# The last product with A taken by rows, and B split for the second pair already, in a two-block FFN kernel

## The chip, the cores and the metric

The kernel runs on one core of a Trainium2 chip. The metric is the device time of one execution in microseconds (us); the time of a version is the median of its runs. An execution is one launch that reads the inputs from HBM and leaves the output there.

## What is computed

The input x has 32 samples of 64 channels and 1024 positions. Two blocks follow one another, each of the form x + ffn(cond(x)). cond is four one-dimensional convolutions with styled weights (same, up, same, down). The first ffn is a gated mixture of low-rank experts, the second a dense layer with 4-bit weights:

```
def block0(x):                        # tokens: 2048 rows of 1024
    t = cond0(x, style)
    scores = t @ Wr.T                                  # 64 experts
    G = softmax of the 16 largest scores, 0 elsewhere
    h = einsum('nd,krd->nkr', t, A) * G[:, :, None]    # 64 experts x rank 16 = 1024
    return x + 2.0 * einsum('nkr,kdr->nd', h, B)
def block1(x):
    t = cond1(x, style)
    return x + t @ (scales * q - zeros) + bias
```

The change lies where block 0 passes from its product with A (and Wr) to its product with B.

## The kernel before, in words

**Pairs.** Two samples of 64 channels fill the 128 partitions, so there are 16 pairs. Three long loops run over them. The first (`for k in range(NP)`) makes the convolutions of block 0 for pairs ahead, and in `layer0` the product of pair k's tokens with A and Wr, the gates, and the gated h, which goes to DRAM (`hgd`). The second (`for p in range(NP)`) loads h of each pair, turns it with transposes (`turned_h`), multiplies it with B and adds the residual (`layer0b`). The third does block 1.

**Whole and split.** A product is done in one of two forms. In whole form it is an fp32 matmul; the profile has two records for each. In split form both sides are cut into an upper part (the top bits, `high`, L148) and a lower part, and three fp32r matmuls are summed: Q is upper x upper plus lower x lower, and D the product of the crossed parts (td = th - tl of the tokens, L872, and `crossed_weights` of the weights, L373). `joined` puts Q and D together. `WHOLE = (0, 1)` names the pairs that go in whole form, in both loops: the weights are loaded plain, and are split while pairs 0 and 1 run. Q and D each need a PSUM bank of their own, so a pair in split form holds two banks per chunk of columns, a whole one only one.

**Splitting the weights.** `split_weights` (L358 to L369) takes row k of the weights (128 of the 1024 contraction rows). For each half of its columns: a high on DVE (L148, into a tile of tag `hi`, of which there are three), the lower part by a subtraction on POOL (L365), and a copy of the high on ACT (L366); then, for the row, the crossing on DVE (L373). The result for row k lies in block k of the pool `wts`; A's split rows (`wa`), B's (`wb`) and others share these eight blocks, so row k of `wb` can be written only when row k of `wa` has been read for the last time. B itself comes plain into `cv` (`load_b`), over rooms that the convolutions of block 0 have left.

**Order.** The framework that assembles the kernel takes the instructions in the order of the program, with a place further ahead for what is ready earlier by its own estimate, fixes one queue per engine and sets the semaphores. Each engine then works its queue in that order. `tc.issue_after(x)` puts instructions behind x on x's engine. `layer0` and `layer0b` are generators: what stands between two `next(main)` in the loops is put between two parts of the product.

**Around the change.** In the last round of the first loop (pair 15) the product with A runs chunk by chunk: Q of chunks 0 and 1, D of both with the gates behind chunk 0, then chunk 2 (L973 to L999). Chunks 0 and 1 fill the four banks of tag `fps`, and chunk 2 takes two of these again. Then come the last three rows of B and the transposes of pair 0's h (L1330, L1331). In the second loop pairs 0 and 1 run whole from the plain B (`braw`), and `split_weights` is called for rows 0 to 3 in the first round and 4 to 7 in the second (L1365, L1366). Pair 2 is the first to use `wb`. The transposes pass through the three banks of tag `cps`. For the pairs from 2 on `turned_h` also makes tl and scales it (L864), and `crossed` makes td behind the pair before. `load_residual` fetches x of a pair: for whole pairs into a tile of tag `tl`, for others into `cv` at `O_Y + Y`, which overlaps rows 5 and 6 of the plain B.

Of the kernel before, what the change touches and what calls it, by code (L numbers as in the profile page):

```python
# [20 lines left out]
NP = B // 2  # L21
L = 1024
HL = L // 2
HQ = HL // 2 + 1
NC = L // P
H = 512
E = 64
# [35 lines left out]
def adaln_ffn_kernel(ctx: ExitStack, tc: tile.TileContext, t, out: bass.AP):  # L63
    nc = tc.nc
# [19 lines left out]
    def fpst(name):  # L84
        return fps.tile([P, H], F32, tag="fps", name=name)
# [66 lines left out]

    done, tbl, outers, uppers = {}, {}, {}, {}
    WHOLE = (0, 1)
    DIRECT = 4


# [744 lines left out]
    def layer0(p, ws):  # L902

        hs = wk.tile([P, AW], F32, tag="w4", name=f"hs{p}", bufs=3)
        key = f"x0_{p}"
        whole = p in WHOLE

        def joined(col, w, qd):
            dst = hs[:, col : col + w]
            if whole:  # L910
                nc.scalar.copy(dst, qd[0])
                return
            nc.scalar.activation(dst, qd[0], AF.Copy, scale=1.0 + 1.0 / RADIX)
            nc.vector.scalar_tensor_tensor(dst, qd[1], -1.0 / RADIX, dst, ALU.mult, ALU.add)

        ga = tiny.tile([P, E], F32, tag="ga", name=f"ga_{p}")

        def gates():
            s0 = hs[:, :E]
            m0 = tiny.tile([P, 8], F32, tag="m0", name=f"m0_{p}")  # L920
            m1 = tiny.tile([P, 8], F32, tag="m1", name=f"m1_{p}")
            s1 = tiny.tile([P, E], F32, tag="s1", name=f"s1_{p}")
            s2 = tiny.tile([P, E], F32, tag="s2", name=f"s2_{p}")
            nc.vector.max(m0, s0)
            nc.vector.match_replace(s1, m0, s0, LOW)
            nc.vector.max(m1, s1)
            nc.vector.match_replace(s2, m1, s1, LOW)
            nm = tiny.tile([P, 1], F32, tag="nm", name=f"nm_{p}")
            nc.vector.tensor_scalar_mul(nm, m0[:, 0:1], -1.0)
            ex = tiny.tile([P, E], F32, tag="ex", name=f"ex_{p}")  # L930
            nc.scalar.activation(ex, s0, AF.Exp, bias=nm)
            su = tiny.tile([P, 1], F32, tag="su", name=f"su_{p}")
            nc.vector.scalar_tensor_tensor(ga, s2, LOW, ex, ALU.is_equal, ALU.mult)
            nc.vector.reduce_sum(su, ga, axis=AX.X)
            nc.vector.reciprocal(su, su)  # L935
            done["gates"] = nc.vector.tensor_scalar_mul(ga, ga, su)

        def gated(c):
            a, b = CHUNKS[c]
            v = hs[:, E + a * R : E + b * R].rearrange("p (e r) -> p e r", r=R)  # L940
            g = ga[:, a:b].unsqueeze(2).to_broadcast([P, b - a, R])
            nc.gpsimd.tensor_tensor(v, v, g, ALU.mult)

        def chunk(c):
            a, b = CHUNKS[c]
            w = (b - a) * R + (E if c == 0 else 0)
            col = a * R + (E if c > 0 else 0)
            banks = [fpst(f"h{p}_{c}_{j}")[:, :w] for j in range(1 if whole else 2)]
            return banks, slice(col, col + w)

        def done_with(c, ch):
            product(ch, key, ws, at, D)
            joined(ch[1].start, ch[1].stop - ch[1].start, ch[0])

        if whole:

            three = [chunk(c) for c in range(3)]
            ks = (2, 3, 4, 5, 0, 1, 6, 7)
            for n, k in enumerate(ks):
                for ch in three:  # L960
                    product(ch, key, ws, at, Q, (k,), ks[0], ks[-1])
                if n in (0, 1, 2, 3, 5):
                    yield
            for c, ch in enumerate(three):
                done_with(c, ch)
            gates()
            yield
            for c in range(3):
                gated(c)
            nc.sync.dma_start(hgd[p], hs[:, E:])  # L970
            return

        two = []  # L973

        ks = tuple(range(6 if p == len(WHOLE) else NC))
        for c in range(2):
            two.append(chunk(c))
            product(two[c], key, ws, at, Q, ks)
            yield
        for c in range(2):  # L980
            if p == len(WHOLE):
                product(two[c], key, ws, at, D, ks)
            else:
                done_with(c, two[c])
                if c == 0:
                    gates()
            yield
        if p == len(WHOLE):
            for c in range(2):
                product(two[c], key, ws, at, Q, (6, 7))  # L990
                product(two[c], key, ws, at, D, (6, 7))
                joined(two[c][1].start, two[c][1].stop - two[c][1].start, two[c][0])
                if c == 0:
                    gates()
        ch = chunk(2)
        product(ch, key, ws, at, Q)
        yield
        done_with(2, ch)
        yield  # L999
        for c in range(3):  # L1000
            gated(c)
        nc.sync.dma_start(hgd[p], hs[:, E:])
# [4 lines left out]
        return hg  # L1007

    def turned_h(p, hg):
        whole = p in WHOLE  # L1010
        key = f"h{p}"
        th = tokens("th", f"th{key}", F32 if whole else F32R)
        toks[key] = [th] if whole else [th, tokens("tl", f"tl{key}")]
        for g in range(2):
            ps = cpst(f"ht{p}_{g}")
            for c in range(4):
                k = 4 * g + c
                nc.tensor.transpose(  # L1018
                    ps[:, c * P : (c + 1) * P], hg[:, k * P : (k + 1) * P], ident
                )  # L1020
            ks = slice(4 * g, 4 * g + 4)

            def d(v):
                return v[:, ks].rearrange("p a b -> p (a b)")

            if whole:
                nc.scalar.copy(d(th), ps)
            else:
                split(ps, lambda v: v, d(th), d(toks[key][1]), f"hh{p}_{g}")
        if not whole:  # L1030
            scaled_low(toks[key][1])
# [1 line left out]
    residual = {}  # L1033

    def load_residual(p):
        if p in WHOLE:
            v = tokens("tl", f"xres{p}", F32).rearrange("p a b -> p (a b)")
        elif p < NP - 1:
            v = cv[:, O_Y + Y : O_Y + Y + L]
        elif p < NP:  # L1040
            v = wk.tile([P, L], F32, tag="w4", name="xres", bufs=3)
        else:
            return
        nc.sync.dma_start(v, t["x"][p])
        residual[p] = v

    def layer0b(p, ws):

        whole = p in WHOLE
        key = f"h{p}"  # L1050
        xres = residual.pop(p)
        x1 = wk.tile([P, L], F32, tag="w4", name=f"x1_{p}", bufs=3)
# [20 lines left out]
        if p == NP - 1:  # L1073
            qds = [banks(c) for c in range(2)]

            for part in (Q, D):
                for k in range(4):
                    for ch in zip(qds, cols):
                        product(ch, key, ws, lambda k: k, part, (k,))
            yield  # L1080
            for ch in zip(qds, cols):
                product(ch, key, ws, lambda k: k, Q, range(4, NC))
                yield
            for c, ch in enumerate(zip(qds, cols)):
                product(ch, key, ws, lambda k: k, D, range(4, NC))
                joined(c, qds[c])
                if c == 0:
                    yield
        else:
            qds = [banks(c) for c in range(2)]  # L1090
            for ch in zip(qds, cols):
                product(ch, key, ws, lambda k: k, Q)
            for c, ch in enumerate(zip(qds, cols)):
                product(ch, key, ws, lambda k: k, D)
                joined(c, qds[c])
                yield
        if p not in WHOLE:
            load_residual(p + 1)
        nc.sync.dma_start(x1d[p].rearrange("p f j -> p (f j)"), x1)
        v = x1.rearrange("p (f j) -> p f j", f=4)  # L1100
# [185 lines left out]
    for k in range(NP):  # L1286
# [4 lines left out]
            outer_of(k + 2)  # L1291
        if last:
            hg = load_h(0)
        main = layer0(k, araw if k in WHOLE else wa)
        next(main)
        if k == 0:
# [28 lines left out]
        for fs in beside:  # L1325
            for f, *v in fs:
                f(*v)
            next(main)
        if last:
            load_b(range(5, NC), braw)  # L1330
            turned_h(0, hg)  # L1331
        elif k + 1 in WHOLE:
            outer(k + 1)
        if k + 2 < NP and k not in WHOLE:
            weights(k + 2)
# [8 lines left out]
        if not last:  # L1344
            crossed(f"x0_{k + 1}")

    hg = load_h(1)
    set1 = factors(1, cv[:, : 3 * AW], cv[:, 3 * AW : O_Y + Y])
    qw = None
    for p in range(NP):  # L1350
        if p + 1 < NP:
            turned_h(p + 1, hg)
        if p + 2 < NP:
            hg = load_h(p + 2)
        if p == NP - 1:
# [2 lines left out]
            tables_of(NP + 2)  # L1358
            outer_of(NP + 1)
            begin(NP + 1)  # L1360
        if p <= len(WHOLE):
            load_residual(p)
        main = layer0b(p, braw if p in WHOLE else wb)
        next(main)
        if p in WHOLE:  # L1365
            split_weights(braw, L, range(4 * p, 4 * p + 4), wb, "wb")  # L1366
        if p == 7:
            clear(1)
            clear_y([yv(0)])
# [112 lines left out]
```

## Time and profile before

| what | value |
|---|---|
| median of 3 runs | 908.21 us (907.2 to 909.05) |
| the profiled execution | 907.35 us, of which the span on the page is 905.3 us |
| granted TensorE clock over the span | 0.999 |
| pair 14's last product with A ends | 390.09 us |
| pair 15's product with A | 390.09 to 401.94 us |
| product with B, pairs 0 and 1 (whole) | 404.03 to 417.76 and 418.64 to 432.4 us |
| first and last subtraction for wb (POOL, L365) | 401.43 and 440.88 us |
| last crossing for wb (DVE, L373) ends | 442.14 us |
| pair 2 (the first in split form) | 433.0 to 446.5 us |
| pair 3 starts | 449.27 us |

Times within the profile are counted from the start of the span. PE is TensorE, PEld its weight loads, DVE is VectorE, ACT ScalarE, POOL GpSimd, SP the engine that issues most transfers. A row of a timeline gives the start, the length, the engine, the source line, the operation and its tiles; in brackets stands how long the engine had been idle before, and what ended that. The chain of waits goes back from the last instruction to whatever released each step.

### The profile page before, as it was taken

How to read it: one execution, taken by the hardware profiler on the slowest of the kernel's cores; microseconds unless marked ns; L12 is line 12 of the kernel's file. 1: busy time of each engine (PE TensorE's matmuls, PEld its weight loads, DVE VectorE, ACT ScalarE, POOL GpSimd, SP SyncE). 2: the span in 40 equal slices, each digit the busy share in tenths (PEclk: the TensorE clock that was granted, in tenths of full speed). 3: DMA queues.
4: the chain of work that ended last, by engine and by line, in shares of the span. 5: the costliest groups of instructions: out<-in, count | busy, mean ns of one | idle time of the engine just before them, and what ended most of it. 6: DMA issues, size and time to landing. Idle time of an engine off the chain costs nothing.

```text
span 905.3 us, 14844 instructions
## 1 busy us (share of the span) xinstructions
PE 876.4 (97%) x5133; PEld 785.8 (87%) x5133; DVE 707.1 (78%) x1450; ACT 328.4 (36%) x717; POOL 467.2 (52%) x603
## 2 busy tenths in 40 slices
PE   5999999999999999999899999999999999999997
PEld 4877789999999999994688888788899999999997
DVE  4565888888888888577986666569998899999986
ACT  6435433333333444333332221247233323333230
POOL 7325654444444444456571222433776767676673
PEclk9999999999999999999999999999999999999999
DMA  8521232222222222345376664456433243334311
GB/s 247 144 72 53 54 99 73 79 77 77 76 77 76 76 77 71 113 168 160 129 228 209 220 197 153 176 191 187 148 110 114 89 129 115 107 110 118 118 65 70
DMA packets 49738, 109.81 MB, mean 121 GB/s; under 512 B 13700, under 2 KB 22400, under 8 KB 49664
## 3 DMA queue, kind: packets, MB, share of 16 engines
q1 hardware_dynamic: 48704, 107.88, 38.3%
q10 hardware_dynamic: 960, 0.99, 0.5%
q8 instruction: 41, 0.67, 0.3%
q14 instruction: 33, 0.27, 0.1%
HBM read 70.97 MB, written 37.88 MB: 120 GB/s over the span
## 4 chain that ended last, share of the span: by engine, by line
PE 75%; DVE 12%; issue 5%; POOL 4%; DMA 2%; ACT 1%; DVEq 0%; POOLq 0%; ACTq 0%; SPq 0%
PE h L892 16%; PE o L892 15%; PE q L1143 12%; PE r L781 6%; PE f L608 6%; PE r L812 5%; PE c L732 5%; PE r L789 3%; PE g L585 2%; PE c L727 2%; DMA x1e<-dd 1%; PE ht L1018 1%; DVE cv L694 1%; DVE x L1063 1%; POOL wa L365 1%
## 5 line engine op out<-in xcount | busy, mean ns | idle before, releaser
L697 POOL TENSOR_TENSOR cv<-cv 128x256 f32<-128x256 f32 x120 | 77.8, 648 | 123.7 <-DVE su L935 72.6
L694 DVE TENSOR_TENSOR cv<-cv 128x257 f32<-128x257 f32 x120 | 99.7, 863 | 1.2 <-ACT cv L717 1.0
L729 ACT ACTIVATE yt<-c,be,al 128x257 f32<-128x257 f32 x56 | 31.7, 565 | 120.4 <-PE c L727 109.3
L1143 PE MATMUL q<-wq,thx 128*128 128x342 f32 x384 | 73.0, 331 | 1.6 <-ACT thx L850 1.6
L631 POOL TENSOR_TENSOR cv<-cv 128x256 f32<-128x256 f32 x60 | 56.1, 934 | 33.8 <-ACT cv L626 33.8
L1143 PE MATMUL q<-wq,tlx 128*128 128x342 f32 x384 | 72.4, 330 | 0.0
L892 PE MATMUL h<-wa,tdx 128*128 128x352 f32 (+1 forms) x336 | 71.9, 350 | 0.2 <-DVE wa L373 0.2
L797 DVE TENSOR_TENSOR rt<-r,tbl 128x256 f32<-128x256 f32 x60 | 25.1, 418 | 56.1 <-PE r L789 56.0
L608 PE MATMUL f<-gs,iw 128*128 128x128 f32 (+1 forms) x384 | 68.2, 327 | 0.2 <-issue 0.2
L781 PE MATMUL r<-cv 128*128 128x128 f32 x480 | 66.7, 282 | 0.9 <-POOL cv L631 0.5
L608 PEld LDWEIGHTS f<-gs,iw 128*128 128x128 f32 x384 | 61.8, 190 | 5.9 <-issue 0.5
L781 PEld LDWEIGHTS r<-cv 128*128 128x128 f32 x480 | 63.5, 196 | 3.3 <-POOL cv L631 1.8
L872 POOL TENSOR_TENSOR tdx<-thx,tlx 128x1024 fp32r<-128x1024 f32 x14 | 35.5, 2538 | 57.6 <-ACT tlx L864 48.1
L892 PE MATMUL h<-wa,thx 128*128 128x352 f32 (+1 forms) x336 | 64.7, 333 | 0.0
L1143 PEld LDWEIGHTS q<-wq,thx 128*128 128x128 f32 x384 | 60.3, 189 | 3.6 <-ACT thx L850 2.7
L812 PE MATMUL r<-cv 128*128 128x128 f32 x480 | 63.4, 274 | 0.0
L1143 PEld LDWEIGHTS q<-wq,tlx 128*128 128x128 f32 x384 | 61.9, 189 | 0.8
L892 PE MATMUL h<-wa,tlx 128*128 128x352 f32 (+1 forms) x336 | 62.4, 327 | 0.0
L892 PE MATMUL o<-wb,thh 128*128 128x512 f32 x224 | 59.8, 400 | 2.6 <-ACT wb L366 1.6
L623 ACT COPY cv<-f 128x256 f32<-128x256 f32 x64 | 23.9, 374 | 100.5 <-PE f L608 90.1
L892 PEld LDWEIGHTS h<-wa,tdx 128*128 128x128 f32 x336 | 56.9, 188 | 2.3 <-DVE wa L373 0.4
L812 PEld LDWEIGHTS r<-cv 128*128 128x128 f32 x480 | 58.3, 191 | 0.0
(304 smaller groups left out, 2124.6 us busy)
## 6 DMA issues: line engine op xcount, KB each, us to landing
cv<-in_x_dram SPq DMA_DIRECT2D x60, 256.0 KB
cv<-x1e SPq DMA_DIRECT2D x64, 192.5 KB
x1e<-dd SPq DMA_DIRECT2D x16, 514.0 KB
hgd<-hs SPq DMA_DIRECT2D x16, 512.0 KB
hg<-hgd SPq DMA_DIRECT2D x16, 512.0 KB
x1d<-x SPq DMA_DIRECT2D x16, 512.0 KB
xb<-x1d SPq DMA_DIRECT2D x16, 512.0 KB
out_dram<-o SPq DMA_DIRECT2D x15, 512.0 KB
```

The source lines that it names most:

```text
L608: done["f"] = nc.tensor.matmul(pv[:, n : n + 2 - k], iw[:, e].rearrange("p a b -> p (a b)"), v, start=(m == 0), stop=(m == len(steps) - 1) ...
L631: nc.gpsimd.tensor_tensor(f[:, 4 * P : 6 * P].rearrange("p (a b) -> p a b", b=P), v[:, :, 0], v[:, :, 1], ALU.add,)
L694: nc.vector.tensor_tensor(d[:, k], yo[:, k : k + HQ], yb, ALU.subtract)
L697: nc.gpsimd.tensor_tensor(e[:, :, k], d[:, :, 2 * k : 2 * k + HQ - 2 : 2], d[:, :, 1 : HQ - 1 : 2], ALU.subtract)
L729: nc.scalar.activation(yt, mid, AF.Identity, bias=be0[:, n : n + 1], scale=a)
L732: done["c"] = nc.tensor.matmul(ps, w[:, q], xe[:, o : o + w_], start=True, stop=True)
L781: nc.tensor.matmul(ps[:, j * P : (j + 1) * P], y[:, j + k : j + k + 2 * P - 1 : 2], w(4 + k), start=(k == 0), stop=(k == 1),)
L789: nc.tensor.matmul(ps[:, (2 + j) * P : (3 + j) * P], d[:, j, 1 : HQ - 1 : 2], w(6 + j), start=True, stop=True,)
L812: done["r"] = nc.tensor.matmul(ps[:, j * P : (j + 1) * P], y[:, YE + (2 * q + k) * P : YE + (2 * q + k + 1) * P], w(q + 2 * k), start=True ...
L872: done["td"] = nc.gpsimd.tensor_tensor(*(v.rearrange("p a b -> p (a b)") for v in (td, *toks[key])), ALU.subtract)
L892: nc.tensor.matmul(banks[l == 2], toks[key][l][:, order(k)], w[:, cols], start=(k == first and l != 1), stop=(k == last and l in (2, min(n ...
L1143: nc.tensor.matmul(ps, half[:, k], wq[at(k)][:, c * QC : (c + 1) * QC], start=(k == 0 and j == 0), stop=(k == NC - 1 and j == 1),)
```

## The change

B is now split for pair 1 too: `WHOLEB = (0,)` takes the place of `WHOLE` in the second loop, so that only pair 0 runs whole there. The rows of B are split in three goes, in the order `ROWS` = 5, 6, 0, 1, 2, 3, 4, 7:

- rows 5, 6 and 0 right behind the first loop;
- rows 1 and 2 in the same place of the program, their DVE part behind the last gates;
- rows 3, 4 and 7 in the first round of the second loop, their DVE part behind the lower parts of pair 1's tokens.

Pair 15's product with A goes by rows: all three chunks at once, in four banks of `fps` and two of `cps`; Q of the first three rows, D of these, then Q and D of three rows more, then rows 4 and 7 chunk by chunk with the joins, and the gates behind chunk 0. Pair 1's product with B takes Q by rows in the same order, both halves of the columns together in four banks. The last loads of B and the transposes of pair 0's h move ahead of pair 15's product.

```diff
@@ -152,6 +152,8 @@
 
     done, tbl, outers, uppers = {}, {}, {}, {}
     WHOLE = (0, 1)
+    WHOLEB = (0,)
+    ROWS = (5, 6, 0, 1, 2, 3, 4, 7)
     DIRECT = 4
 
 
@@ -941,11 +943,11 @@
             g = ga[:, a:b].unsqueeze(2).to_broadcast([P, b - a, R])
             nc.gpsimd.tensor_tensor(v, v, g, ALU.mult)
 
-        def chunk(c):
+        def chunk(c, bank=fpst):
             a, b = CHUNKS[c]
             w = (b - a) * R + (E if c == 0 else 0)
             col = a * R + (E if c > 0 else 0)
-            banks = [fpst(f"h{p}_{c}_{j}")[:, :w] for j in range(1 if whole else 2)]
+            banks = [bank(f"h{p}_{c}_{j}")[:, :w] for j in range(1 if whole else 2)]
             return banks, slice(col, col + w)
 
         def done_with(c, ch):
@@ -964,6 +966,32 @@
             for c, ch in enumerate(three):
                 done_with(c, ch)
             gates()
+            yield
+            for c in range(3):
+                gated(c)
+            nc.sync.dma_start(hgd[p], hs[:, E:])
+            return
+
+        if p == NP - 1:
+            three = [chunk(0), chunk(1), chunk(2, cpst)]
+
+            def part(ch, limbs, ks):
+                product(ch, key, ws, at, limbs, ks, ROWS[0], ROWS[-1])
+
+            for limbs in (Q, D):
+                for k in ROWS[:3]:
+                    for ch in three:
+                        part(ch, limbs, (k,))
+                yield
+            for k in ROWS[3:6]:
+                for ch in three:
+                    part(ch, Q + D, (k,))
+                yield
+            for c, ch in enumerate(three):
+                part(ch, Q + D, ROWS[6:])
+                joined(ch[1].start, ch[1].stop - ch[1].start, ch[0])
+                if c == 0:
+                    gates()
             yield
             for c in range(3):
                 gated(c)
@@ -1007,7 +1035,7 @@
         return hg
 
     def turned_h(p, hg):
-        whole = p in WHOLE
+        whole = p in WHOLEB
         key = f"h{p}"
         th = tokens("th", f"th{key}", F32 if whole else F32R)
         toks[key] = [th] if whole else [th, tokens("tl", f"tl{key}")]
@@ -1033,7 +1061,7 @@
     residual = {}
 
     def load_residual(p):
-        if p in WHOLE:
+        if p in WHOLEB:
             v = tokens("tl", f"xres{p}", F32).rearrange("p a b -> p (a b)")
         elif p < NP - 1:
             v = cv[:, O_Y + Y : O_Y + Y + L]
@@ -1046,7 +1074,7 @@
 
     def layer0b(p, ws):
 
-        whole = p in WHOLE
+        whole = p in WHOLEB
         key = f"h{p}"
         xres = residual.pop(p)
         x1 = wk.tile([P, L], F32, tag="w4", name=f"x1_{p}", bufs=3)
@@ -1088,13 +1116,19 @@
                     yield
         else:
             qds = [banks(c) for c in range(2)]
-            for ch in zip(qds, cols):
-                product(ch, key, ws, lambda k: k, Q)
+            if p == len(WHOLEB):
+
+                for k in ROWS:
+                    for ch in zip(qds, cols):
+                        product(ch, key, ws, lambda k: k, Q, (k,), ROWS[0], ROWS[-1])
+            else:
+                for ch in zip(qds, cols):
+                    product(ch, key, ws, lambda k: k, Q)
             for c, ch in enumerate(zip(qds, cols)):
                 product(ch, key, ws, lambda k: k, D)
                 joined(c, qds[c])
                 yield
-        if p not in WHOLE:
+        if p not in WHOLEB:
             load_residual(p + 1)
         nc.sync.dma_start(x1d[p].rearrange("p f j -> p (f j)"), x1)
         v = x1.rearrange("p (f j) -> p f j", f=4)
@@ -1291,6 +1325,8 @@
             outer_of(k + 2)
         if last:
             hg = load_h(0)
+            load_b(range(5, NC), braw)
+            turned_h(0, hg)
         main = layer0(k, araw if k in WHOLE else wa)
         next(main)
         if k == 0:
@@ -1326,10 +1362,7 @@
             for f, *v in fs:
                 f(*v)
             next(main)
-        if last:
-            load_b(range(5, NC), braw)
-            turned_h(0, hg)
-        elif k + 1 in WHOLE:
+        if k + 1 in WHOLE:
             outer(k + 1)
         if k + 2 < NP and k not in WHOLE:
             weights(k + 2)
@@ -1344,12 +1377,18 @@
         if not last:
             crossed(f"x0_{k + 1}")
 
+    split_weights(braw, L, ROWS[:3], wb, "wb")
+    with tc.issue_after(done["gates"].ins):
+        split_weights(braw, L, ROWS[3:5], wb, "wb")
     hg = load_h(1)
     set1 = factors(1, cv[:, : 3 * AW], cv[:, 3 * AW : O_Y + Y])
     qw = None
     for p in range(NP):
         if p + 1 < NP:
             turned_h(p + 1, hg)
+        if p == 0:
+            with tc.issue_after(done["lo"].ins):
+                split_weights(braw, L, ROWS[5:], wb, "wb")
         if p + 2 < NP:
             hg = load_h(p + 2)
         if p == NP - 1:
@@ -1358,12 +1397,10 @@
             tables_of(NP + 2)
             outer_of(NP + 1)
             begin(NP + 1)
-        if p <= len(WHOLE):
+        if p <= len(WHOLEB):
             load_residual(p)
-        main = layer0b(p, braw if p in WHOLE else wb)
+        main = layer0b(p, braw if p in WHOLEB else wb)
         next(main)
-        if p in WHOLE:
-            split_weights(braw, L, range(4 * p, 4 * p + 4), wb, "wb")
         if p == 7:
             clear(1)
             clear_y([yv(0)])
```

## Prediction

> **What bounds the kernel now.** I read the page first, for the engine that holds the whole; then the chain of waits cut to 360 to 500 us, where the change lies; then, in that stretch, the groups that write the split weights (tile wb) and the timelines of TensorE (PE), VectorE (DVE) and GpSimd (POOL).
>
> ```profile
> PE 876.4 (97%) x5133; PEld 785.8 (87%) x5133; DVE 707.1 (78%) x1450; ACT 328.4 (36%) x717; POOL 467.2 (52%) x603
> ...
> PE 75%; DVE 12%; issue 5%; POOL 4%; DMA 2%; ACT 1%; DVEq 0%; POOLq 0%; ACTq 0%; SPq 0%
> ```
>
> PE is busy for 97% of the span, so a step pays only if it shortens PE's work or one of its few pauses. The chain shows where it is not PE that carries:
>
> ```profile
> 402.10 1.92 PE ht L1018 x16
> 404.03 13.73 PE o L892 x32
> 417.76 0.87 PE ht L1018 x8
> 418.64 7.74 PE o L892 x18
> ...
> 427.33 2.24 POOL wb L365
> ...
> 429.61 2.30 POOL tdh L872
> ...
> 440.92 0.06 DVE wb L373
> ...
> 449.27 11.13 PE o L892 x48
> ```
>
> Pairs 0 and 1 of the product with B take 13.73 us each in whole form (32 records, 0.429 us apart), a pair in split form 10.91 us (48 records, 0.227 us). From 427 to 449 us the chain has left PE: it runs over the splitting of B and the DVE work queued behind it. PE pauses three times in that stretch:
>
> ```profile
> 435.30 0.50 PE L892 MATMUL o<-wb,thh 128*128 128x512 f32 x1 [0.65 <-ACT wb L366]
> 436.70 0.50 PE L892 MATMUL o<-wb,thh 128*128 128x512 f32 x1 [0.91 <-ACT wb L366]
> ...
> 449.27 2.06 PE L892 MATMUL o<-wb,thh 128*128 128x512 f32 x8 [1.08 <-DVE cv L1062]
> ```
>
> The price of splitting stands in the groups, as shortest/middle/longest ns, and in three rows of the timelines:
>
> ```profile
> L365 POOL TENSOR_TENSOR wb<-cv,wbh x16: 1258/1448/2245, 401.4 to 438.8; 128x512 fp32r<-128x512 f32 x16
> L373 DVE SCALAR_TENSOR_TENSOR wb<-wb x8: 1224/2064/3387, 404.6 to 440.9; 128x1024 fp32r<-128x1024 f32 x8
> ```
>
> ```profile
> 412.17 1.23 DVE L373 SCALAR_TENSOR_TENSOR wb<-wb 128x1024 fp32r<-128x1024 f32 x1 [1.16 <-POOL wb L365]
> 429.61 3.39 DVE L373 SCALAR_TENSOR_TENSOR wb<-wb 128x1024 fp32r<-128x1024 f32 x1 [1.16 <-POOL dd L1104]
> ```
>
> ```profile
> 429.57 2.35 POOL L872 TENSOR_TENSOR tdh<-thh,tlh 128x1024 fp32r<-128x1024 f32 x1
> ```
>
> A crossing (L373) takes 1.23 us when POOL stands still and 3.39 us when POOL's td of 2.35 us starts just ahead of it: it stood still for that td and then ran for 1.04. The two engines take turns here.
>
> **Part by part.** PE first, from 390.09, where pair 14's last product ends.
> - turned_h(0) is moved ahead of the last product: its 8 transposes cost 0.87 us in either place; L1018's two pairs together took 1.92.
> - The last product by rows: 72 records as before, 11.85 us (390.09 to 401.94). Rows 5, 6 and 0 are through after 27 of them, 4.4 us, so at 390.96 + 4.4 = 395.4, row 5 after 21, at 394.4. The end is 402.8. Its td is read after 18 records, at 393.9; POOL delivers at 393.07, so the margin is 0.8 us, and cost nothing. Chunk 2 takes two of the three cps banks; pair 1's transposes find one of them only when ACT has emptied it (L913, 0.47 us): 0.5 us. Pair 0 then starts at 402.8 + 0.87 + 0.5 = 404.2, and ends at 417.9; with ht of pair 2, pair 1 could start at 418.8.
> - Pair 1 in split form: 10.91 for 13.73, which is 2.8 us less. With nothing in the way PE would do pair 1, ht, pair 2, ht and the sps group (0.81) by 418.8 + 10.91 + 0.87 + 10.91 + 1.68 = 443.2, 6.1 us ahead of 449.27, where pair 3 starts now. That is the most it can bring.
> - What is added: pair 1 now needs its lower limbs: four DVE steps (two hh, two lo, 0.6 us apart in the queue), the scaling on ACT (1.06), and td on POOL (2.4). Its residual is joined in two DVE steps per half, so L1062 comes twice more (0.69 each), behind the product.
> - SP: load_h(0) and B's last three loads are issued in the same order as now, at 385.4 to 386.8 behind the last filters. Pair 0's residual takes the room of the last pair's tl and moves from 388.95 to about 403; a store and the load that waited for it stand 2.67 us apart on SP (408.55, 411.22), so I estimate it lands by 406, ahead of pair 0's first half at 411. Behind it stands the load of pair 2's h, wanted at 417.9. Nothing.
>
> Now the two engines that feed PE. All eight rows must be apart before pair 1 ends, not before pair 2 ends. A row is two highs and a crossing on DVE, two subtractions on POOL. Now rows 0 to 3 go from 401.43 to 417.68, 16.25 us, so 4.06 each; three of their highs had been done early, and the same holds after the change. One rule of the Trainium skill speaks against the change: SBUF — State Buffer, section "Who interferes with whom". It says that a DVE instruction with two SBUF inputs, or in a two-port mode, and a GpSimd instruction that reads SBUF shut each other out for their full length. By that rule a row is the sum of its parts alone, 2 x 1.27 + 2 x 0.41 + 1.23 = 4.6 us; without it POOL alone would count, 2.54. The trace's 4.06 lies near the rule (the early highs explain 0.3). Eight rows are 20.3 us without it, 32.5 by the row, 36.8 by the rule. I take the row.
>
> The order in the queues: the three room tiles for highs (tag hi) are handed out in the order of the program. Now row 4's first high comes at 422.38, right behind the last high of pair 2's tokens at 421.79, though its B row was there and DVE stood idle before the crossing at 416.46 (2.38 us). So the three goes, the gates and pair 1's tokens do not mix freely. Step by step:
> - rows 5, 6, 0 from 394.4: 12.2, to 406.6. In the planned order their crossings stand ahead of the last gates, whose scores exist only from 400.9;
> - the gates, with the joins (L914 to L936 ran from 396.86 to 399.88): 3.0, to 409.6; POOL has nothing to do meanwhile;
> - three gatings on POOL (0.68, 0.82, 0.99) and rows 1, 2: 2.5 + 8.1, to 420.2;
> - pair 1's tokens: 2.4, to 422.6, tl scaled at 423.7. So PE, due at 418.8, stands until about 423.7;
> - rows 3, 4, 7 with td of pair 1 among them: 12.2 + 2.4, to 437.2; row 7's subtraction is ready 1.2 earlier, at 436.0.
>
> PE has rows 5 to 4 behind it by then, does row 7 (two records of the second half wait, 0.45) and all of D, 16 x 0.227 = 3.6: pair 1 ends at 440.1, against 432.4 now. Then ht 0.87, pair 2 10.91 without its present stalls, 1.68: pair 3 starts at 453.6. That is 4.3 us later than 449.27. What was late there now, the join on DVE (L1062), is no longer late, as DVE is done with B 5 us earlier than now (442.14).
>
> Behind 449 nothing gives it back: from 449 to 632 us PE's pauses over 0.3 us are 0.54, 1.51, 0.75 and 1.27, each behind work of the same pairs. The gates' delay touches only pair 15's store, wanted 14 pairs later.
>
> Bounds of what the trace does not show. The wait for the order in the queues: 0 (gates and tokens run beneath POOL's subtractions) to 5.4 (3.0 + 2.4); I take all, since the highs that POOL needs stand behind them. A long pause of PE: the skill's TensorE: Matmul & The Clock Gate, Part 1, says that an idle window of about 3.4 us halves the clock until as long a busy stretch has passed; the granted clock is 1.00 in all windows of this stretch, but its longest pause is 1.08. By the rule the 4.7 us pause could cost up to 1.7 us, by the trace nothing; I take nothing and keep 1.7 in the range.
>
> **The rivals.** *Overlap holds.* Drop the 5.4: the last crossing ends at 431.8, pair 1 at 434.7, pair 3 starts at 448.2, 1.1 us earlier than now: 907.1 us. The point that decides is 432.9 for the last crossing. With POOL at its undisturbed 2.54 a row, all is ready by 394.4 + 20.3 + 2.5 + 2.4 = 419.6, and the full 6.1 come: 902.1. For it: DVE's token steps read PSUM, so need no turn. Against it: rows 0 to 3 now show the turns.
>
> *The bank.* A pair in split form holds four banks and by rows it needs the second half's bank at its second group. That bank is the one pair 0's first half filled by 411, and DVE freed it at 417.60 only, behind row 3's crossing. If that join (L1063) stands behind the third go's highs, it ends at about 434.8; then 30 records of Q and 16 of D, 10.4: pair 1 ends at 445.2, 917.6 in all. For it: exactly that order now. Against: ACT's casts leave DVE a hole early in the third go. If the rows are not released early at all, the result is much the same: first go 8 us later, less the 3.0 of the gates.
>
> **How the numbers follow.** The profiled execution took 907.35 us, span 905.3 and 2.05 around it; 905.3 + 4.3 + 2.05 = 911.7. The median of the runs is 908.21, 0.86 above, so I predict 912.5. About 0.2%, 1.8 us, is what a measurement can tell from no change. Chances: forecast (1.8 to 6.5 us slower) 0.47; bank or no early release (over 6.5) 0.18; overlap in part (within 1.8) 0.17; overlap that gains more 0.18. So slower 0.65, same 0.17, faster 0.18. The range, 904.5 to 918, leaves about 0.1 below, among the full gains, and under 0.1 above.
>
> **What would show it.** Right: the last L373 of wb ends near 437, pair 1's first matmul near 423.7, pair 3's near 453.6, POOL idle for some 3 us before the last gatings, L373's mean still near 2.0 us. Wrong: gates ending before 405 with the first go still under way; L373's mean near 1.3; pair 1 starting by 419 without a pause, or its second half waiting for L1063 (the bank).

## The result, and the profile after

| | before | after |
|---|---|---|
| median of 4 runs | 908.46 us (907.2 to 909.05) | 917.78 us (915.95 to 920.53) |
| ratio to before | | 1.0105 (95%: 1.0085 to 1.0125) |
| profiled execution, its span | 907.35, 905.3 us | 916.22, 914.1 us |
| last crossing for wb ends | 442.14 us | 437.10 us |
| pair 1, 2, 3 start, from the mark | 32.5, 47.0, 63.3 us | 36.2, 57.6, 70.3 us |
| PE's last matmul ends, from the mark | 514.9 us | 523.8 us |

The changed kernel is 9.3 us slower by the medians, 8.9 by the two profiles; 4.3 were forecast. The mark is the start of pair 14's last product with A (386.0 us in before, 385.9 in after). The profiled executions of the kernels below reach it up to 3 us apart (385.9 to 388.8 us), so they are compared from there; a median holds the part ahead of the mark too. The difference is about 1%, with an interval clear of no change.

The page's line of busy engines for the changed kernel:

```profile
PE 877.0 (96%) x5149; PEld 790.4 (86%) x5149; DVE 707.5 (77%) x1456; ACT 329.9 (36%) x718; POOL 470.2 (51%) x604
```

PE is busy for as long as before (877.0 to 876.4 us). Pair 1 in split form should have taken 2.8 us off; matmuls that took longer have filled that up (see the clock below). The other 8.2 of the 8.8 us by which the span grew are PE standing still. The chain of waits of the changed kernel from 426 to 476 us says behind what:

```profile
426.96 3.35 POOL tdh L874
430.31 1.23 POOL wb L367
...
435.87 1.23 DVE wb L375
437.10 0.60 DVE dd L1139
437.70 0.60 DVE dd L1141
438.30 1.20 DVE hh L148 x2
...
440.69 0.88 DVE cv L208
...
442.81 0.61 DVE cv L1090
443.56 11.16 PE o L894 x48
...
470.30 2.89 DVE dd L1141
473.19 0.88 DVE cv L271
```

(Lines are those of the changed file: L367 and L375 are L365 and L373 of before, L1090 is L1062.) Up to the last crossing it is the forecast's path, with td of pair 1 between two rows on POOL. Behind it the chain does not go to PE, as the forecast had it, but on through DVE's queue: the edges of pair 0 (dd), the tokens of pair 2 (hh and tl), four steps on the filters of block 1 (L208 to L211), and only then the join L1090 that frees the bank for pair 2. PE's timeline in the same stretch:

```profile
431.59 0.49 PE L894 MATMUL o<-wb,tlh 128*128 128x512 f32 x1 [1.99 <-POOL wb L367]
433.84 0.80 PE L894 MATMUL o<-wb,thh 128*128 128x512 f32 x1 [1.75 <-ACT wb L368]
...
436.48 5.17 PE L894 MATMUL o<-wb,tdh 128*128 128x512 f32 x16
...
443.56 2.09 PE L894 MATMUL o<-wb,thh 128*128 128x512 f32 x8 [1.03 <-DVE cv L1090]
...
474.11 0.23 PE L338 MATMUL rows<-ident,cv 64*32 64x64 f32 x1 [1.69 <-DVE cv L271]
```

PE pauses four times in this stretch. The first two are rows of B that come late, within pair 1. Behind them D's 16 records take 5.17 us where 3.79 is usual. The third is the join. The fourth, 30 us on, had no counterpart in before. Why D was slow stands in the column PEclk (after POOL's) of the windows:

```profile
432.50:439.35 6.85, 5.48 (x11) 3.57 (x12) 5.43 (x9) 4.97 (x14) 4.18 (x16) 0.50 0.30 115
439.35:446.00 6.65, 5.62 (x29) 4.50 (x29) 6.55 (x12) 2.33 (x5) 1.50 (x3) 1.00 0.49 158
```

The granted clock was 0.50 in the first window and 1.00 on either side of it. PE worked for 5.48 us at half clock, which by my estimate is 2.7 us more than that work takes at full clock: the 2.8 us that pair 1 saved.

How often the two engines met in the split rows shows in the instructions that touch wb (shortest/middle/longest ns):

```profile
L367 POOL TENSOR_TENSOR wb<-cv,wbh x16: 1262/1339/2272, 394.6 to 434.6; 128x512 fp32r<-128x512 f32 x16
L375 DVE SCALAR_TENSOR_TENSOR wb<-wb x8: 1225/1226/2309, 397.3 to 435.9; 128x1024 fp32r<-128x1024 f32 x8
```

The middle crossing fell from 2.06 to 1.23 us: most now find POOL at rest, since DVE waits for POOL instead. A row became hardly cheaper by it: rows 5, 6 and 0 took from 394.6 to 406.35, so 3.9 us each, where 4.06 were forecast.

### The profile page after: what moved, and what is told of

The parts are those of the page before. It is cut to its first block, busy times and chain, and to the rows that moved or that the text cites. A ratio compares the mean times of both kernels' runs of the same rounds, so it can differ in the third digit from the quotient of the medians.

```text
span 914.1 us, 14897 instructions
## 1 busy us (share of the span) xinstructions
PE 877.0 (96%) x5149; PEld 790.4 (86%) x5149; DVE 707.5 (77%) x1456; ACT 329.9 (36%) x718; POOL 470.2 (51%) x604
## 4 chain that ended last, share of the span: by engine, by line
PE 41%; DVE 7%; POOL 2%; issue 2%; DMA 1%; ACT 1%; DVEq 0%; POOLq 0%; SPq 0%; ACTq 0%
PE o L894 13%; PE q L1177 12%; PE r L783 3%; PE f L610 3%; PE r L814 3%; PE c L734 2%; PE r L791 1%; PE c L729 1%; PE g L587 1%; POOL tdh L874 1%; DVE x L1091 1%; PE ht L1046 1%; DMA x1e<-dd 1%; DVE nib L427 1%; DVE cv L1090 1%
## 5 line engine op out<-in xcount | busy, mean ns | idle before, releaser
L894 PE MATMUL h<-wa,tdx 128*128 128x352 f32 (+1 forms) x336 | 73.9, 351 | 0.2 <-DVE wa L375 0.2
L894 PE MATMUL o<-wb,thh 128*128 128x512 f32 x240 | 66.3, 402 | 2.8 <-ACT wb L368 1.8
L610 PE MATMUL f<-gs,iw 128*128 128x128 f32 (+1 forms) x384 | 68.2, 327 | 0.2 <-issue 0.2
L894 PE MATMUL h<-wa,thx 128*128 128x352 f32 (+1 forms) x336 | 67.7, 334 | 0.0
L894 PE MATMUL o<-wb,tlh 128*128 128x512 f32 x240 | 64.2, 394 | 2.8 <-POOL wb L367 2.0
L783 PEld LDWEIGHTS r<-cv 128*128 128x128 f32 x480 | 63.6, 196 | 2.8 <-POOL cv L633 1.8
L894 PE MATMUL h<-wa,tlx 128*128 128x352 f32 (+1 forms) x336 | 65.3, 327 | 0.0
L874 POOL TENSOR_TENSOR tdx<-thx,tlx 128x1024 fp32r<-128x1024 f32 x14 | 35.5, 2538 | 57.6 <-ACT tlx L866 48.1
L1090 DVE SCALAR_TENSOR_TENSOR cv<-o,cv 128x512 f32<-128x512 f32 x28 | 19.4, 691 | 57.6 <-PE o L894 57.6
```

Of the source, the lines that this page charges most:

```text
L610: done["f"] = nc.tensor.matmul(pv[:, n : n + 2 - k], iw[:, e].rearrange("p a b -> p (a b)"), v, start=(m == 0), stop=(m == len(steps) - 1) ...
L783: nc.tensor.matmul(ps[:, j * P : (j + 1) * P], y[:, j + k : j + k + 2 * P - 1 : 2], w(4 + k), start=(k == 0), stop=(k == 1),)
L874: done["td"] = nc.gpsimd.tensor_tensor(*(v.rearrange("p a b -> p (a b)") for v in (td, *toks[key])), ALU.subtract)
L894: nc.tensor.matmul(banks[l == 2], toks[key][l][:, order(k)], w[:, cols], start=(k == first and l != 1), stop=(k == last and l in (2, min(n ...
L1090: nc.vector.scalar_tensor_tensor(v, qd[1], -SCALING / RADIX, v, ALU.mult, ALU.add)
```

## Experiments

Theory T (turns and queue): DVE and POOL hold each other up while B is split, which makes a row cost 4 us; pair 1 in split form wants all rows earlier than that, and what is queued on DVE behind the last crossing then sets when pair 2 starts. Rivals: the half clock of PE made the loss; or the order of goes, gates and tokens; or pair 1 in split form as such. Here is all that ran, from the mark:

| run | median us | ratio to before, same chip | pair 1 | pair 2 | pair 3 | PE's end |
|---|---|---|---|---|---|---|
| before | 906.9, 907.5, 907.0 | 1 | 32.5 | 47.0 | 63.3 | 514.9 |
| after | 917.78 | 1.0105 (1.0085 to 1.0125) | 36.2 | 57.6 | 70.3 | 523.8 |
| e1 pair 1 whole | 917.35 | 1.0112 (1.0087 to 1.0136) | 35.8 | 51.0 | 73.9 | 526.6 |
| e1b same, third go later | 917.62 | 1.0126 (1.0104 to 1.0148) | 35.7 | 50.9 | 72.7 | 524.2 |
| e10 same, in pair 1's round | 907.41 | 1.0000 (0.9989 to 1.0010) | 35.7 | 50.3 | 62.9 | 514.3 |
| e2 subtraction on DVE | 905.50 | 0.9982 (0.9968 to 0.9996) | 32.3 | 47.9 | 60.6 | 511.8 |
| e3 before, subtraction on DVE | 904.13 | 0.9963 (0.9954 to 0.9972) | 32.5 | 47.0 | 59.6 | 510.7 |
| e4 PE filled | 915.88 | 1.0102 (1.0074 to 1.0130) | 36.2 | 57.7 | 71.8 | 524.2 |
| e5 tokens first | 914.60 | 1.0077 (1.0052 to 1.0103) | 35.7 | 55.7 | 68.3 | 519.5 |
| e6 filter steps a round later | 915.62 | 1.0099 (1.0082 to 1.0115) | 36.2 | 57.6 | 69.4 | 522.3 |
| e7 e2 and e5 | 906.12 | 0.9987 (0.9975 to 0.9999) | 32.3 | 48.1 | 60.8 | 512.4 |
| e8 filter steps behind a join | 918.57 | 1.0122 (1.0104 to 1.0140) | 36.2 | 56.5 | 69.2 | 524.0 |
| e9 e8 and e4 | 914.47 | 1.0080 (1.0063 to 1.0097) | 36.2 | 55.6 | 68.2 | 519.2 |
| e11 e2 and e8 | 906.19 | 0.9983 (0.9975 to 0.9991) | 32.3 | 47.9 | 60.5 | 512.9 |

The starts and ends are from one profile of each kernel.

**e2: the turns taken away.** One line of `split_weights`:

```
-                nc.gpsimd.tensor_tensor(ws[:, 1, cs], raw[k][:, cs], h, ALU.subtract)
+                eng = nc.vector if name == "wb" else nc.gpsimd
+                eng.tensor_tensor(ws[:, 1, cs], raw[k][:, cs], h, ALU.subtract)
```

> The changed kernel with the lower parts of B subtracted on DVE in place of POOL; A's stay on POOL. Theory (turns): without turns a row costs DVE about 2 x 0.33 + 2 x 0.6 + 1.14 = 3.0 us instead of 4.1, although DVE gets 16 more instructions; the last crossing moves from 437 to about 427, pair 3 starts near 445, 904 to 908 us. Rival (order of the queues: gates and tokens between the goes): DVE is the queue that holds everything and gets 10 us more work, so it gets no faster: 917 us or more. Rival (clock): no statement of its own.

As T had it: PE ends 12.0 us earlier than in the changed kernel, and the median is 1.4 us below before. Pair 1 starts at 32.3 instead of 36.2, and pair 3 9.7 us earlier. DVE took over 11.7 us of work and was still done sooner: the last crossing ends at 43.6 from the mark, where the changed kernel has 51.2.

**e3: the same line in the kernel before.**

> The kernel before, with one edit: the subtraction that makes the lower part of B's rows runs on DVE instead of POOL. Pair 1 stays whole, the last product with A stays chunk by chunk. Theory of turns (DVE and POOL hold each other up in the splitting of B, and DVE's queue behind the last crossing sets pair 3's start): with POOL out of it, the last crossing ends 5 us or more before 442.14, the pauses of 0.65, 0.91 and 1.08 us ahead of pair 3 go, pair 3 starts at 445.5 to 447.5 instead of 449.27, and the time is 1.5 to 3.5 us below the kernel before on the same chip, some 903.5 to 905.5. Then the gain of the changed kernel with the same edit over the kernel before (1.6 us) is none of the change's own. Rival (POOL is only short of throughput, or the gain came from pair 1 in split form): DVE, with 0.7 us more per half row, is the later engine; no gain, 907 or more.

The groups that split B, from 380 to 470 us (busy us, mean ns of one, idle before), first in before, then in e3:

```profile
L365 POOL TENSOR_TENSOR wb<-cv,wbh 128x512 fp32r<-128x512 f32 x16 | 25.0, 1585 | 5.3 <-issue 4.9 <-DVE wbh L148 0.4
L373 DVE SCALAR_TENSOR_TENSOR wb<-wb 128x1024 fp32r<-128x1024 f32 x8 | 15.8, 1974 | 5.9 <-POOL wb L365 4.7 <-POOL dd L1104 1.2
L148 DVE TENSOR_SCALAR wbh<-cv 128x512 int32<-128x512 int32 x16 | 14.3, 927 | 2.9 <-POOL wb L365 2.9
...
L366 DVE TENSOR_TENSOR wb<-cv,wbh 128x512 fp32r<-128x512 f32 x16 | 11.4, 744 | 1.1 <-PE h L893 1.1
L374 DVE SCALAR_TENSOR_TENSOR wb<-wb 128x1024 fp32r<-128x1024 f32 x8 | 9.7, 1216 | 0.0
L148 DVE TENSOR_SCALAR wbh<-cv 128x512 int32<-128x512 int32 x16 | 9.2, 608 | 0.0
```

In before, highs and crossings keep DVE busy for 30.1 us and the subtractions keep POOL busy for another 25.0. In e3 all three are on DVE and take 30.3 us there. That a POOL too slow by itself was the cause does not fit this: then DVE's own instructions would not have become shorter (a crossing 1.97 to 1.22 us, a high 0.93 to 0.61). The chain of e3 holds nothing but PE from 395 to 495 us. So the gain of e2 is none of the change's: the same edit is worth at least as much without it (0.9963 to 0.9982, with intervals that touch; pair 3 at 59.6 to 60.6). e3 has the lowest median of all versions.

Why the change gives nothing even there shows in one window of e2 (the span of pair 1; PE, PEld, DVE, ACT and POOL busy), with two rows of the timelines in it:

```profile
418.00:434.00 16.00, 13.78 (x62) 10.02 (x60) 16.00 (x22) 8.32 (x20) 6.40 (x16) 1.00 0.38 136
...
417.89 2.62 POOL L875 TENSOR_TENSOR tdh<-thh,tlh 128x1024 fp32r<-128x1024 f32 x1 [8.73 <-DMA cv<-in_cw_dram]
418.17 3.13 DVE L148 TENSOR_SCALAR wbh<-cv 128x512 int32<-128x512 int32 x2
```

DVE is busy for 16.00 of 16.00 us. Yet 2.4 us of that is standing still: two highs take 3.13 us beside POOL's td of pair 1, where the two ahead of them took 0.75. So one turn, that of td, is left in e2. PE pauses five times, 2.2 us in sum, and pair 1 lasts 15.7 us to pair 2's start, where the whole form takes 14.5.

**e4: the half clock taken away.** Fillers on PE, results never read:

```
+                fill = mpst(f"fill{p}")
                 for k in ROWS:
+                    if k in (4, 7):
+                        for m in range(8):
+                            nc.tensor.matmul(fill, toks[key][0][:, 5], ws[5][:, 0, :H], start=(m == 0), stop=(m == 7))
```

> The changed kernel with 8 more matmuls (128x512, sums that nobody reads) in front of row 4 and 8 in front of row 7 of pair 1's product, so that TensorE is not idle while it waits for these rows. Theory (turns): the last crossing stays near 437.1; only the halved clock of 432.5 to 439.3 us goes, D of pair 1 takes 3.6 instead of 5.0 us: 914.5 to 917 us. Rival (clock): the halved clock makes most of the loss of 9 us: 912 us or less.

D is back at 3.85 us, and nothing is won: the wait for the join grows from 1.03 to 2.60 us, and pair 2 starts at 57.7 (57.6 in the changed kernel). Behind that longer pause PEclk falls to 0.51 in pair 2, which makes pair 3 later still. The half clock within pair 1 lay wholly beside DVE's queue.

**e6 and e8: the filter steps out of that queue.** e6 delays the generator that makes them (`if 1 < p < 7`, the last part doubled); e8 keeps the join's last instruction in `joined` and binds them behind it:

```
+            done["joined"] = nc.vector.scalar_tensor_tensor(
...
+        with tc.issue_after(done["joined"].ins) if i else nullcontext():
             nc.vector.tensor_tensor(sq, cwr, cwr, ALU.mult)
```

> The changed kernel, with the part of the next layer's filter factors that stands in DVE's queue behind the last crossing (2.1 us of DVE in round 1) made five rounds later instead. Theory (pair 2 waits for what is queued on DVE behind the last crossing, not for pair 1's product or the half clock): pair 2 starts 0.5 to 2 us earlier than 443.56, its wait of 1.03 us gone, as pair 1's product ends at 441.5 and the transposes at about 442.4; total 0.7 to 2 us lower, 915.5 to 917. Rival (the half clock or PE sets the start): pair 2 starts at 443.3 to 443.8 as now and the time is unchanged, 917 to 918.

> The changed kernel, with the four DVE steps on the next layer's filters (2.1 us), which stand between the last crossing and pair 1's joins, bound behind pair 2's joins; the run before this one with that aim left them where they were. Times from the start of pair 14's last product with A: there pair 2 starts at 57.6 us in the changed kernel, the last crossing ends at 51.2. Theory (DVE's queue behind the last crossing sets pair 2's start): the join comes at 51.2 + 1.2 + 2.4 = 54.8 and no longer counts; pair 2 follows PE's own work, half clock and all, at about 56.5. So pair 3 starts about 1.1 us earlier than 70.3, 915.5 to 917. Rival (half clock and PE's own work alone): pair 2 at 57.6 as before, no change.

e6 missed its aim: its edit moves the parts by one round, not by five, and the framework put L208 to L211 into the same place all the same, and pair 2 started at 57.6. Its 0.9 us at pair 3 come from the filters' matmuls (L228, 0.81 us), which moved from ahead of pair 3 to ahead of pair 4. e8 did what T said up to pair 3: 56.5 and 69.2, each 1.1 us earlier. Then it was given back: L272 (L271 of after) ended late again, PE paused 1.89 us, and the clock fell to 0.54 for 476 to 479 us. In time it is no better than the changed kernel.

**e9: both.**

> The same, and 16 idle matmuls (results never read) in the two pauses of PE within pair 1, so that the clock stays up. With the fillers alone pair 2 still started at 57.7. Theory (two waits side by side, DVE's queue and the half clock; either alone hides the other): with both gone pair 2 starts at 55.0 to 55.8, 2 us earlier than in the changed kernel, pair 3 at about 68, near the forecast's 453.6 less 386 = 67.6; total 914 to 916. If only DVE's queue counted, it is as the run without fillers, 56.5 and 915.5 to 917.

```profile
438.22 3.79 PE L895 MATMUL o<-wb,tdh 128*128 128x512 f32 x16
...
443.43 2.08 PE L895 MATMUL o<-wb,thh 128*128 128x512 f32 x8 [0.54 <-DVE cv L1091]
```

Pair 2 starts at 55.6 and pair 3 at 68.2: two waits lay side by side, and either hid the other. From the mark, PE ends 4.4 us behind before, close to the forecast's 4.3. The median is still 7.5 us above that of before: this profile reached the mark 1.9 us later than that of before did, and whether that is chance or comes with the kernel stays open. The pause behind L271 is gone here too, though nothing was done about it (see below).

**e5 and e7: the order of goes and tokens.** The go behind the gates is dropped and rows 1 and 2 join the third:

```
-    with tc.issue_after(done["gates"].ins):
-        split_weights(braw, L, ROWS[3:5], wb, "wb")
...
-                split_weights(braw, L, ROWS[5:], wb, "wb")
+                split_weights(braw, L, ROWS[3:], wb, "wb")
```

> The changed kernel with rows 1 and 2 put into the third go, so that pair 1's tokens stand ahead of them on DVE right behind the gates. Theory (turns): pair 1 can start sooner, before 420 to 421 us, where pair 0 ends, but the last crossing stays within 1 us of 437.1, so the time does too: 915.5 to 919 us. Rival (order): what delays is the tokens' place, 2.4 us and more, and pair 1's start at 423.5: 913 us or less.

> The changed kernel with two edits together: B's lower-part subtraction on DVE, and rows 1 and 2 in the third go, behind pair 1's tokens, instead of behind the gates. If the two costs are apart (turns, and the order of the queues), the gains add: 905.5 less up to 3 us, 902.5 to 905. If the tokens came late only because the goes ahead of them were slow (turns), the second edit has nothing left to give, and as the rows come later it may cost some tenths: 905 to 907.

e5 fell between the theories. Pair 1 starts only 0.5 us earlier, because PE is through with pair 0 no sooner than in the changed kernel; within pair 1 it still waits for rows (1.62, 1.74, 0.32 us), and the clock halves there as well. But the last crossing ends 2.0 us sooner from the mark, at 49.2, and pairs 2 and 3 come 2.0 us earlier with it, the 6.5 us of DVE's queue behind it unchanged. The pause behind L271 is missing here too. With the turns gone (e7) the order is worth nothing, 0.2 us the wrong way. So 2.0 us of the loss were the order, and only because the rows were dear.

**e1, e1b and e10: rows early, pair 1 whole.** `WHOLEB = (0, 1)`; e1b puts the third go behind pair 0's first join, e10 into pair 1's round, where before has rows 4 to 7. The last product by rows and the early goes are left of the change, and Q by rows falls to pair 2.

> The changed kernel with pair 1 again in whole form in the product with B; the last product with A by rows and the three goes stay. Theory (turns): the loss comes from pair 1 needing all of split B before DVE and POOL, taking turns, have it. Then with pair 1 whole the split is wanted only by pair 2, near 436 us, after the last crossing (near 433): the loss goes, 906.5 to 910 us. Rival (the rows): the product by rows in six banks and the early goes themselves delay PE (pair 1's transposes wait for banks): then most of the loss stays, 914 us or more. Rival (clock): like the first, with the granted clock at 1.00 throughout, since PE has no long pause.

> The changed kernel with pairs 0 and 1 whole as before, and the third go put behind pair 0's first join in the program, so that less of pair 0's joins stands behind the last crossing. Only the product with A by rows and the early rows of B are then left of the change. Theory of turns: the last crossing ends at 433 to 436, 6 us or more before pair 2 needs it; if pair 1's residual is loaded in time, pair 3 starts at 447.5 to 449 and the time is 905.5 to 908. If a join of pair 0 still stands behind the last crossing, that load is late again and the wait for it takes the place of the one removed: 911 to 917.

> The changed kernel with pairs 0 and 1 whole, and the third go of rows (3, 4, 7) where the kernel before splits rows 4 to 7, in pair 1's round, so that pair 0's joins don't stand behind it. What is left of the change is the last product with A by rows and five rows of B apart early. Theory: three rows at 4.9 us each from 422 end at 436 to 437, the joins behind them by 444, and pair 2 and 3 run without a pause: pair 3 starts at 60 to 61 from the same mark, where the kernel before has 63.3; 904.5 to 906.5 (before on the same chip 907 to 907.5). So rows early pay, and pair 1 in split form is what costs. Rival (the turns take back what is won early): 907 or more.

e1 and e1b missed. The last crossing did end early (433.39 us in e1), but pair 0's second join stands behind it on DVE; the room of its residual is that of pair 1's residual, whose load was issued only at 436.76 us. DVE's timeline of e1:

```profile
444.45 1.09 DVE L1091 SCALAR_TENSOR_TENSOR x<-o,xres 128x512 f32<-128x512 f32 x1 [6.47 <-DMA xres<-in_x_dram]
450.95 0.96 DVE L208 TENSOR_TENSOR cv<-cv 128x768 f32<-128x768 f32 x1 [5.40 <-DMA cv<-in_cw_dram]
```

Two loads in a row stop DVE, and PE behind it for 5.93 us. e10 is free of that, and shows what early rows are worth: from pair 2's start to pair 3's it takes 12.7 us, not 16.3 as in before. Nearly all of it was lost ahead: pair 1 starts at 35.7 instead of 32.5. The chain of e10 shows how:

```profile
405.16 0.07 DVE wb L375
...
406.31 0.53 DVE hs L916
...
407.56 0.35 ACT ex L933
407.91 0.37 ACT hs L915
...
408.33 0.66 PE ht L1046 x4
```

By rows, all three chunks of pair 15 end together. Their joins (L916) stand behind row 0's crossing on DVE, the exponential of the gates behind the joins, and the emptying of the last `cps` banks (L915) behind that on ACT. PE pauses 1.09 us ahead of pair 0 and 1.83 within it, and did not in before. With the subtraction on DVE (e2) neither pause is there.

**e11: e2 with e8's edit.**

> The changed kernel with B's lower-part subtraction on DVE (alone 905.5, pair 2 at 47.9 and pair 3 at 60.6 from the same mark, DVE busy for all of pair 1), and the four filter steps behind pair 2's joins. Theory (with the turns gone DVE's own work is the bound from pair 1's start to pair 2's): 2.1 us less in DVE's queue take 0.6 to 0.9 us off, pair 2 at 47.0 to 47.4, and the time is 904.2 to 905.0, no better than the kernel before with the subtraction on DVE (904.1). Rival (PE and ACT set it): unchanged, 905.5.

No effect, pair 2 at 47.9: in e2 the four steps had their place behind pair 1's first join already. That DVE is the bound stays likely (15.47 us busy of 15.5 in the same window), but this run does not show it; 2.4 us of it are again two highs that stand beside td (3.13 us).

## Why the prediction was wrong in size

Right, with what was measured against what was forecast: first go done 406.35 us (406.6), gates 409.7 (409.6), rows 1 and 2 419.8 (420.2), tokens 422.2 (422.6), row 7's last subtraction 435.84 (436.0), last crossing 437.10 (437.2). The turns, the order in the queues and the sign were as argued. In the last go there was some luck: rows 3, 4 and 7 took 11.6 us without td (12.2), and td took 3.35 (2.4). The bank rival did not happen, although its 917.6 is close to the result: PE never waited for pair 0's joins, which ran at 425.8 and 433.4; the second half's bank was free. Nor did "Overlap holds".

- **The step that failed**: "What was late there now, the join on DVE (L1062), is no longer late, as DVE is done with B 5 us earlier than now (442.14)." It compared an earlier crossing with an unchanged need. But the join that counts is now one pair earlier too: pair 1's, ahead of pair 2. Behind the last crossing DVE's queue holds 6 to 7 us in both kernels: 7.1 to pair 3's start in before (442.14 to 449.27), 6.5 to pair 2's in after (437.10 to 443.56). The sum is then 5.0 earlier, 0.7 less of queue, and one pair of 12.9 us more behind it: pair 3 at 456.44, 7.2 later than 449.27, where 4.3 were forecast. The half clock lies beneath the same wait: PE, slowed by it, stood only 1.03 us for the join, and with a full clock would have stood 2.60 (e4). e9 shows that the two together are most of the missing part: without them pair 3 starts at 68.2 from the mark, forecast 67.6.
- **"Behind 449 nothing gives it back"**: nothing did, but something was added. At 470.30 the step dd (L1141) took 2.89 us instead of 0.68, because POOL's td had begun just ahead of it, and PE stood 1.69 us for L271 behind it:

```profile
469.79 2.85 POOL L874 TENSOR_TENSOR tdh<-thh,tlh 128x1024 fp32r<-128x1024 f32 x1
```

  In before td began at 465.36, when both dd were through, and in e9 at 470.25, when the second dd was under way. In e4, e6 and e8 a dd of 2.32, 2.27 and 2.83 us beside td stands ahead of the same pause (1.11, 1.06 and 1.89 us). It is one more turn, decided by half a microsecond: 1.7 us.
- **PE ahead of pair 1**: 0.5 us were forecast for the `cps` bank; 1.17 and 1.82 were measured. It cost nothing here, as pair 1's tokens were later still, but in e10 it ate nearly the whole gain. The 0.5 counted ACT's emptying alone, not that it stands behind the exponential, and that behind DVE.
- **The clock**: the Trainium skill's page TensorE: Matmul & The Clock Gate, Part 1, gives an idle window of about 3.4 us. The forecast took nothing for it, and expected one pause of 4.7 us, which PE's own lateness had cut to 0.4 and 0.8. In fact 1.99 and 1.75 us with one matmul between them halved the clock for 6.85 us, and in e8 a single 1.89 us did; here less than the page's window was enough. D lost 1.4 us by it, all of it hidden (e4), but hidden beneath the very wait that the forecast had left out.
- **L373's mean near 2.0** was wrong too: 1.51. The turns moved to where DVE waits for POOL, and the 4.06 us of a row nearly held all the same (3.9). That rate was the right thing to take, not the instruction's mean.

So there are 4.3 us forecast, 2.9 more at pair 3 from DVE's queue with the half clock beneath it, and 1.7 from a late turn: together the profiles' 8.9. (2.9 is by the chain, 456.44 to 453.6; by the table's starts it is 2.7, since a row of PE's timeline begins up to 0.24 us before the one ahead of it ends.) The 0.4 up to the medians' 9.3 lie within their spread.

What stays open: which step of DVE bounds pair 1 once the subtractions are off POOL, and what the turn of td that is left there costs (e2, e11). No run took the late turn at L271 away by itself; it was gone by chance in e5 and e9. And no run has the last product by rows without the early goes.

## What to carry to other kernels

When a step's deadline moves one iteration forward, go through everything queued behind its last instruction once more: the queue moves with it, and an iteration more stands behind it. Where two engines take turns, try the work on one of them, even the busier one, before the schedule is changed: here one line was worth 3.4 us in the kernel before, and the schedule nothing. Pauses that lie side by side must be removed together to see what either is worth.

## What the hardware showed beyond that

- A subtraction of 128x512 took 0.74 us on DVE and 1.26 to 2.27 on POOL; moved to the engine that was 78% busy, it shortened the kernel.
- The granted clock fell to about a half behind pauses of 1.89 us alone (e8, for about 3.4 us), 2.60 us (e4: 0.51 from 443.5 to 447), 5.93 us (e1: 0.51 for 10.4 us). In the changed kernel 1.69 us alone, and 1.17 and 1.82 us with 2.4 us of work between, left it at 1.00.
- td, 2.35 to 2.40 us for these pairs in before, took 3.35 us at 426.96 in the changed kernel, in the middle of the splitting.
